# Routing from sums of tokens, scalings gathered in the output's stage, and a reordered first group: a fused audio layer on one core

## Chip, cores, metric

One core of a Trainium2 chip. The metric is the device time of one execution in microseconds (us). All runs quoted for a time were fast, that is, none was over 1.5% above the fastest of its kernel.

## The reference, cut

Sixty-four recordings of 80,000 samples are cut into 157 frames of 512, turned by a cosine transform, and pass one layer: an attention-like mixing with a gate, then a mixture of 16 experts, where each recording takes one expert, chosen from the mean of its tokens. All is fp32.

```python
h = einsum('bfh,kh->bfk', frames, dct)                      # 64 x 157 x 512
x = layernorm(h)
#   phases from tanh(x @ Wk), tanh(x @ Wq); V = x @ Wv; causal sums; gate = sigmoid(x @ Wg)
h = h + x + (gate * total + (1 - gate) * pos) / norm @ Wo + bo
x = layernorm(h)
scores = softmax(mean(x, axis=1) @ Wg + bg)                 # over tokens, then route
idx = argmax(scores); gate = scores[idx]
h = h + gate * (x @ We[idx] + be[idx])
```

## The kernel before

The kernel works through 16 groups of four recordings. A group's tokens are five tiles of 128 (the last is called TAIL); the frames lie turned in `xT` (feature by token). A stage of one group runs beside stages of its neighbours: the value stage of group g holds the routing of g-1, the expert stage of g-1 holds the embedding of g+1.

The frames are turned into values without layernorm's division by the deviation. So each token's column of `xT` must be multiplied by its 1/deviation (`rstd`) before the projections. `rstd` has one value per partition (token); a transpose of it, repeated 128 times, puts it along the free dimension of all partitions ("spread"), and VectorE multiplies ("scale"):

```python
# cut below: s = S[g] (the tiles of group g) and blank lines
def spread(g, n, room=None):
    s["by", n] = tr = bank()[:, :P] if room is None else room
    nc.tensor.transpose(tr, s["rstd", n].to_broadcast([P, P]), ident)

def scale(g, n):
    x, tr = tile_of(s["xT"], n), s.pop(("by", n))
    nc.vector.tensor_tensor(x, x, tr.unsqueeze(1).to_broadcast([P, C, P]), ALU.mult)

def expert(g, n, between=lambda c: None, spreads=()):       # 4 chunks of 4 recordings
    ps = psum()
    for c in range(C):
        between(c); expert_chunk(g, n, c, ps[:, 0, :])
    between(C)
    for k, m in enumerate(spreads):
        spread(g + 2, m, ps[:, 1, P * k : P * (k + 1)])
    expert_out(g, n, ps[:, 0, :])
    for m in spreads:
        scale(g + 2, m)
```

The routing multiplies every token by the routing weights and sums afterwards:

```python
def route(g):
    s["each"] = ps = bank()
    for c in range(C):
        for b in range(GB):                                  # four recordings, four column groups
            nc.tensor.matmul(ps[Q*b : Q*(b+1), :L], rwg[:, c, :], s["x2T"][:, c, b, :L],
                             start=(c == 0), stop=(c == C - 1))
def route_sum(g):
    nc.vector.tensor_reduce(tot, s.pop("each")[:, :L], AX.X, ALU.add)
```

PSUM, into which TensorE writes its products, is used as a ring of four buffers of two banks. Line numbers in the profile lines are those of each kernel's own text; below, the transposes of `rstd` are L290 before and L296 after, their scalings on VectorE L296 and L835 before and L302 after, experts L785 and L814, routing L691 and L706, attention's read L605 and L611. In a line of TensorE, `128*32` is rows and columns of the weights, `128x512` the data that stream past them, `x32` how many instructions are merged; what stands in brackets is the idle time before it and who ended it.

## Time and profile before

| | before |
|---|---|
| time, median | 1418.8 us |
| TensorE busy | 99% |
| VectorE, GpSimd, ScalarE busy | 71%, 42%, 28% |
| one group's period | 85.84 us |
| of it value, gate, expert, read and output stage | 21.79, 16.38, 24.02, 23.65 us |

TensorE is never free in the steady groups; the last two rows are distances between first instructions of stages on TensorE. The lines themselves are in the prediction.

### The profile page before, as it was taken

To read this page: it belongs to the slowest core of one execution; us is meant where nothing else is said; L and a number is where in the kernel's file an instruction comes from. 1 tells how busy PE (TensorE), PEld (TensorE's weight loads), DVE (VectorE), ACT (ScalarE), POOL (GpSimd) and SP (SyncE) were. 2 spreads that over 40 slices of the span, in tenths; PEclk is the share of its full clock that TensorE was granted. 3 is DMA by queue.
4 is the path that set the end of the run, shared out by engine and by line. 5 is a ranking of instruction groups with operands and counts; after the bars stand their busy time and mean duration, and the time that the engine had idled before them with its cause. 6 is when DMAs were issued, how large, how long until landed. Compare 5 with 4: busy or idle time off the path is not lost.

```text
span 1419.2 us, 26967 instructions
## 1 busy us (share of the span) xinstructions
PE 1404.2 (99%) x10647; PEld 929.9 (66%) x10647; DVE 1002.4 (71%) x2091; ACT 401.5 (28%) x690; POOL 602.9 (42%) x846
## 2 busy tenths in 40 slices
PE   9999999999999999999999999999999999999998
PEld 5577575675757667575675757657586675766762
DVE  5777776767767676777777767677676777767574
ACT  2414242141422314232142422314223142421410
POOL 2354534535544255533535445255442545335312
PEclk9999999999999999999999999999999999999999
DMA  6013205032140323204132040322303232030305
GB/s 219 1 38 126 75 1 182 20 127 75 51 139 12 132 69 118 84 1 173 29 127 75 13 173 16 127 75 77 117 8 137 64 126 75 1 141 24 127 8 192
DMA packets 47486, 119.74 MB, mean 84 GB/s; under 512 B 9265, under 2 KB 26177, under 8 KB 39425
## 3 DMA queue, kind: packets, MB, share of 16 engines
q0 software_dynamic: 11072, 71.31, 13.0%
q1 hardware_dynamic: 35788, 46.06, 11.0%
q8 instruction: 85, 1.39, 0.4%
q10 hardware_dynamic: 500, 0.64, 0.2%
q14 instruction: 41, 0.33, 0.1%
HBM read 97.41 MB, written 20.58 MB: 83 GB/s over the span
## 4 chain that ended last, share of the span: by engine, by line
PE 90%; DVE 3%; POOL 3%; issue 1%; DMA 1%; ACT 1%; SPq 0%; DVEq 0%; POOLq 0%
PE mm L364 27%; PE mm L571 16%; PE mm L785 16%; PE mm L605 9%; PE mm L235 8%; PE mm L681 3%; PE mm L516 3%; PE mm L250 2%; PE mm L252 2%; POOL rstd L227 1%; PE mm L691 1%; PE mm L590 1%; DVE st L222 1%; PE mm L290 1%; POOL rstd L226 1%
## 5 line engine op out<-in xcount | busy, mean ns | idle before, releaser
L226 POOL TENSOR_SCALAR rstd<-mv 128x1 f32<-128x1 f32 x160 | 53.1, 332 | 545.9 <-DVE mv L224 539.6
L785 PE MATMUL mm<-we,x2T 128*32 128x512 f32 x2400 | 273.2, 595 | 0.0
L785 PEld LDWEIGHTS mm<-we,x2T 128*32 128x32 f32 x2400 | 70.3, 109 | 148.6 <-issue 141.3
L97 DVE TENSOR_TENSOR gT<-mm,gT 128x128 f32<-128x128 f32 (+1 forms) x135 | 87.0, 672 | 88.5 <-PE mm L571 87.0
L613 DVE TENSOR_TENSOR gT<-mm,gT 128x320 f32<-128x320 f32 x256 | 116.8, 487 | 20.7 <-PE mm L605 16.2
L605 PE MATMUL mm<-att,v 32*128 32x192 f32 (+2 forms) x2048 | 129.1, 374 | 1.1 <-ACT res_t L279 1.1
L605 PEld LDWEIGHTS mm<-att,v 32*128 32x128 f32 x2048 | 107.1, 187 | 11.7 <-PE mm L605 3.0
L739 POOL DMA_INDIRECT we<-in_we,rows x60 | 64.3, 1072 | 105.1 <-issue 98.0
L97 DVE TENSOR_TENSOR v<-mm,v 128x512 f32<-128x512 f32 x105 | 70.9, 688 | 52.9 <-PE mm L364 52.9
L581 ACT ACTIVATE gT<-gT,hbg 128x320 f32<-128x320 f32 x120 | 59.6, 554 | 169.0 <-DVE gT L97 169.0
L227 POOL TENSOR_TENSOR rstd<-rstd,power 128x1 f32<-128x1 f32 x160 | 98.2, 614 | 13.3
L97 DVE TENSOR_TENSOR res<-mm,res 128x512 f32<-128x512 f32 x96 | 64.4, 684 | 54.1 <-POOL res L621 39.2
L279 ACT ACTIVATE res<-mm,shift,rstd 128x512 f32<-128x512 f32 x64 | 49.8, 778 | 161.9 <-POOL rstd L265 126.3
L668 ACT ACTIVATE x<-res,shift,rstd 128x512 f32<-128x512 f32 x64 | 52.0, 814 | 137.8 <-DVE res L97 121.4
L364 PE MATMUL mm<-t_o,sum 128*128 128x256 f32 x384 | 88.3, 379 | 0.4 <-DVE sum L96 0.4
L364 PE MATMUL mm<-t_v,sum 128*128 128x256 f32 x360 | 86.7, 384 | 0.0
L284 POOL TENSOR_TENSOR res<-res,bo 128x512 f32<-128x512 f32 x64 | 86.3, 1379 | 0.2 <-issue 0.2
L796 DVE SCALAR_TENSOR_TENSOR res<-mm,gate,res 128x512 f32<-128x512 f32 x64 | 48.0, 750 | 49.3 <-PE mm L290 36.3
L364 PEld LDWEIGHTS mm<-t_o,sum 128*128 128x128 f32 x384 | 71.9, 190 | 11.6 <-PE mm L364 0.8
L621 POOL TENSOR_TENSOR res<-res,u 128x512 f32<-128x512 f32 x45 | 55.9, 1269 | 42.1 <-DVE u L97 42.1
L235 PE MATMUL mm<-wv,xT 128*128 128x512 f32 x160 | 72.0, 594 | 0.0
L364 PEld LDWEIGHTS mm<-t_v,sum 128*128 128x128 f32 x360 | 64.8, 190 | 10.7 <-issue 3.5
(200 smaller groups left out, 2770.5 us busy)
## 6 DMA issues: line engine op xcount, KB each, us to landing
xT<-in_frames SPq DMA_DIRECT2D x32, 640.0 KB, 4.6
out<-res SPq DMA_DIRECT2D x248, 64.0 KB, 1.7
out<-res_t SPq DMA_DIRECT2D x62, 32.0 KB, 1.6
out<-res_t SPq DMA_DIRECT2D x62, 26.0 KB
wv<-in_wv SPq DMA_DIRECT2D x2, 512.0 KB, 5.8
wg<-in_wg SPq DMA_DIRECT2D x1, 1024.0 KB
wo<-in_wo SPq DMA_DIRECT2D x1, 1024.0 KB
we<-in_we,rows POOLq DMA_INDIRECT x60, 8.5
```

Source lines behind the costliest of these rows:

```text
L97: add = lambda *x: nc.vector.tensor_tensor(*x, ALU.add)
L226: nc.gpsimd.tensor_scalar(rstd, mv[:, 1:2], EPS, None, ALU.add)
L227: nc.gpsimd.tensor_tensor(rstd, rstd, power, ALU.pow)
L235: nc.tensor.matmul(ps, tile_of(x[:, c], n), w[:, c, :], start=(c == 0), stop=(c == C - 1))
L284: nc.gpsimd.tensor_tensor(r, r, bo, ALU.add)
L364: nc.tensor.matmul(ps[:, b, :], lhs[:, c, P * b : P * (b + 1)], w[:, c, :], start=(c == 0), stop=(c == 1))
L571: nc.tensor.matmul(ps[:, o, :HN], w[:, c, o * P : (o + 1) * P], rhs[:, c], start=(c == 0), stop=(c == 1))
L581: nc.scalar.activation(to, to, AF.Tanh, bias=hbg[:, c : c + 1], scale=0.5)
L605: nc.tensor.matmul(to, s["v", n][q, c * P : (c + 1) * P], by, start=(n == 0), stop=(n == TAIL))
L613: nc.vector.tensor_tensor(th, r[:, :, n], th, op)
L739: nc.gpsimd.indirect_dma_start(out=ws[b][:, n * k : n * (k + 1)], out_offset=None, in_=of, in_offset=bass.IndirectOffsetOnAxis(ap=rows[:, ...
L785: nc.tensor.matmul(ps[Q * i : Q * (i + 1), :], s["x2T"][:, c, i, Q * n : Q * (n + 1)], s["ws"][i][:, c, :], start=(c == 0), stop=(c == C - 1),
```

## The change

Its intent: take small work off TensorE. (1) VectorE sums each recording's turned tokens, and the routing multiplies two partial sums in place of 157 tokens. (2) The spreads, five a group and lone between expert products, become six transposes in a row in the output stage, with two large scalings. (3) In the first group, gate parts follow each other without spreads between, statistics come ahead of the phasors, and GpSimd's sum of the gate's weights moves back. The last group keeps the token-wise routing (`route_tokens`).

```diff
+    def scale_all(g):
+        ps = psum()
+        lo = 0
+        for n in (0, 1, TAIL, TAIL, 2, 3):
+            rows = slice(0, P) if n != TAIL else slice(0, HT) if lo < HN - 1 else slice(HT, P)
+            ...
+            nc.tensor.transpose(ps[:, m, at : at + w], s["rstd", n][rows].to_broadcast([w, P]), ident[rows, rows])
+            lo += w
+        for m in range(2):
+            x = half(s["xT"], m)
+            nc.vector.tensor_tensor(x, x, ps[:, m, :HN].unsqueeze(1).to_broadcast([P, C, HN]), ALU.mult)
...
+    def token_sum(g, k):
+        lo, hi = ((2 * Q, L), (0, 2 * Q))[k]
+        nc.vector.tensor_reduce(s["xsum"][:, :, k], x[:, :, lo:hi], AX.X, ALU.add)
...
-                    ps[Q * b : Q * (b + 1), :L], rwg[:, c, :], s["x2T"][:, c, b, :L], ...
+                    ps[Q * b : Q * (b + 1), :], rwg[:, c, :], s["xsum"][:, GB * c + b, :], ...
... first_values
-        total = add_up(raw_g, D, "x2T", nc.gpsimd)       # before value(0, 1)
         value(0, 1)
...
+        total = add_up(raw_g, D, "x2T", nc.gpsimd)       # after embed_res(0, 3)
... first_gate: four calls of spread and scale, and the TAIL's, taken out
... project_and_values
         keep_product(g)
+        token_sum(g - 1, 0)
         value_product(g, 6)
         turn_x2(g - 1, 1)
         phasors(g)
         keep_product(g)
-        fold_once(g + 1, 0)      # moves down, to just before value_product(g, 5)
+        token_sum(g - 1, 1)
         value_product(g, 7)
...          # route(g - 1) from before to after value_product(g, 5); value_product(g, 3) ahead of route_spread
... experts_and_embedding
-        expert(g - 1, 0, spreads=(0, 1))
+        expert(g - 1, 0)
-        expert(g - 1, 2, spreads=(2, 3))
+        expert(g - 1, 2)
-        expert(g - 1, 3, spreads=(TAIL,))
+        expert(g - 1, 3)
... attention, after output product 7
+            elif i == 7 and ahead:
+                scale_all(g + 1)
```

More of the change, by code (lines that the diff above doesn't have):

```diff
@@ L284, in add_bo @@
         nc.gpsimd.tensor_tensor(r, r, bo, ALU.add)
-    def spread(g, n, room=None):
+    def scale_all(g):
         s = S[g]
-        s["by", n] = tr = bank()[:, :P] if room is None else room
-        nc.tensor.transpose(tr, s["rstd", n].to_broadcast([P, P]), ident)
-    def scale(g, n):
-        s = S[g]
-        x, tr = tile_of(s["xT"], n), s.pop(("by", n))
-        nc.vector.tensor_tensor(x, x, tr.unsqueeze(1).to_broadcast([P, C, P]), ALU.mult)
+        ps = psum()
+        lo = 0
+        for n in (0, 1, TAIL, TAIL, 2, 3):
+            rows = slice(0, P) if n != TAIL else slice(0, HT) if lo < HN - 1 else slice(HT, P)
+            m, at = divmod(lo, HN)
+            w = rows.stop - rows.start
+            nc.tensor.transpose(
+                ps[:, m, at : at + w], s["rstd", n][rows].to_broadcast([w, P]), ident[rows, rows]
+            )
+            lo += w
+        for m in range(2):
+            x = half(s["xT"], m)
+            nc.vector.tensor_tensor(x, x, ps[:, m, :HN].unsqueeze(1).to_broadcast([P, C, HN]), ALU.mult)
     def quarters(w):
@@ L682, in turn_x2 @@
         copy(s["x2T"][:, :, :, Q * n : Q * (n + 1)], tr.rearrange("p (c b t) -> p c b t", c=C, b=GB))
+    def token_sum(g, k):
+        s = S[g]
+        if k == 0:
+            s["xsum"] = p2.tile([P, C * GB, 2], F32, tag="xsum", name="xsum")
+        x = s["x2T"].rearrange("p c b t -> p (c b) t")
+        lo, hi = ((2 * Q, L), (0, 2 * Q))[k]
+        nc.vector.tensor_reduce(s["xsum"][:, :, k], x[:, :, lo:hi], AX.X, ALU.add)
     def route(g):
         s = S[g]
-        s["each"] = ps = bank()
+        s["each"] = ps = bank()[:, :2]
         for c in range(C):
@@ L691, in route, with route_tokens @@
                 nc.tensor.matmul(
-                    ps[Q * b : Q * (b + 1), :L], rwg[:, c, :], s["x2T"][:, c, b, :L], start=(c == 0), stop=(c == C - 1)
+                    ps[Q * b : Q * (b + 1), :],
+                    rwg[:, c, :],
+                    s["xsum"][:, GB * c + b, :],
+                    start=(c == 0),
+                    stop=(c == C - 1),
+                )
+    def route_tokens(g):
+        s = S[g]
+        s["each"] = ps = bank()[:, :L]
+        for c in range(C):
+            for b in range(GB):
+                nc.tensor.matmul(
+                    ps[Q * b : Q * (b + 1), :], rwg[:, c, :], s["x2T"][:, c, b, :L], start=(c == 0), stop=(c == C - 1)
                 )
@@ L697, in route_sum @@
         s["tot"] = tot = p2.tile([P, 1], F32, tag="tot", name="tot")
-        nc.vector.tensor_reduce(tot, s.pop("each")[:, :L], AX.X, ALU.add)
+        nc.vector.tensor_reduce(tot, s.pop("each"), AX.X, ALU.add)
     def route_spread(g):
@@ L801, in expert_out, with expert @@
                 queue.dma_start(out=out[GB * g + i, Q * n + lo : Q * n + hi, :], in_=o[Q * i + lo : Q * i + hi, :])
-    def expert(g, n, between=lambda c: None, spreads=()):
+    def expert(g, n, between=lambda c: None):
         ps = psum()
@@ L809, in expert @@
         between(C)
-        for k, m in enumerate(spreads):
-            spread(g + 2, m, ps[:, 1, P * k : P * (k + 1)])
         expert_out(g, n, ps[:, 0, :])
-        for m in spreads:
-            scale(g + 2, m)
-    def scale_all(g):
-        s = S[g]
-        ps = psum()
-        for m in range(2):
-            lo = 0
-            for n, w, at in ((0, P, 0), (1, P, 0), (TAIL, HT, 0)) if m == 0 else ((TAIL, HT, HT), (2, P, 0), (3, P, 0)):
-                nc.tensor.matmul(
-                    ps[:, m, lo : lo + w],
-                    s["rstd", n].to_broadcast([P, P]),
-                    ident[:, at : at + w],
-                    start=True,
-                    stop=True,
-                )
-                lo += w
-        for m in range(2):
-            x = half(s["xT"], m)
-            nc.vector.tensor_tensor(x, x, ps[:, m, :HN].unsqueeze(1).to_broadcast([P, C, HN]), ALU.mult)
     def first_values():
@@ L884, in first_values @@
         keep_value(0, 2)
+        next(consts)
+        value(0, 3)
         mean_g = bank()
@@ L887, in first_values @@
         centre(raw_g, mean_g, D)
-        value(0, 3)
         value(0, TAIL)
         keep_value(0, 3)
-        next(consts)
         keep_value(0, TAIL)
@@ L903, in first_values @@
         fold_phases(0)
-        phasors(0, (0,))
-        next(consts)
-        next(consts)
         embed(1, 0)
         embed_statistics(1, 0)
+        next(consts)
+        phasors(0, (0,))
+        embed_res(1, 0)
         phasors(0, (1,))
-        embed_res(1, 0)
+        next(consts)
         next(consts)
@@ L919, in weights @@
             next(made)
-        def deviations(n):
-            spread(1, n)
-            scale(1, n)
         gate_part(0, 0)
@@ L927, in first_gate @@
         embed_statistics(1, 1)
+        weigh()
         embed_res(1, 1)
-        weigh()
         fold_twice(1, 1)
-        deviations(0)
         add_bo(0, 0)
@@ L937, in first_gate @@
         embed_statistics(1, 2)
-        deviations(1)
         embed_res(1, 2)
@@ L947, in first_gate @@
             embed_res(1, n)
-        deviations(2)
         add_bo(0, 2)
@@ L951, in first_gate @@
         gate_part(0, 3)
-        add_bo(0, 3)
-        deviations(3)
-        deviations(TAIL)
-        add_bo(0, TAIL)
+        for n in (3, TAIL):
+            add_bo(0, n)
         weights()
@@ L989, in project_and_values @@
         next(weights, None)
+        fold_once(g + 1, 0)
+        value_product(g, 5)
         route(g - 1)
+        keep_product(g)
         route_sum(g - 1)
-        value_product(g, 5)
-        keep_product(g)
         next(weights, None)
         next(weights, None)
+        value_product(g, 3)
         route_spread(g - 1)
+        keep_product(g)
         pick(g - 1)
@@ L1002, in project_and_values @@
         keep_value(g, TAIL)
-        value_product(g, 3)
-        keep_product(g)
         value_product(g, 4)
@@ L1121, in routes @@
         elif c == 3:
-            route(g)
+            route_tokens(g)
             route_sum(g)
```

## The prediction

> **What bounds the kernel now.** I read the page first: the busy line, then the shares of the chain that ended last.
>
> ```profile
> span 1419.2 us, 26967 instructions
> PE 1404.2 (99%) x10647; PEld 929.9 (66%) x10647; DVE 1002.4 (71%) x2091; ACT 401.5 (28%) x690; POOL 602.9 (42%) x846
> ...
> PE 90%; DVE 3%; POOL 3%; issue 1%; DMA 1%; ACT 1%; SPq 0%; DVEq 0%; POOLq 0%
> ```
>
> TensorE has 15 us without work in the whole span, and the chain runs on it for 90%. So a change pays by the TensorE time that it takes out; what it does to VectorE counts only where VectorE would come late. Busy time of pipelined matmuls overlaps, so I cost a piece of TensorE work as the distance from its start to the start of what follows. The timeline of TensorE, for one group of four samples in the middle (starts in us, durations in us):
>
> ```profile
> 574.76 3.64 PE L785 MATMUL mm<-we,x2T 128*32 128x512 f32 x32
> 578.34 0.71 PE L250 MATMUL mm<-dct_e,xT 128*128 128x128 f32 x4
> ...
> 583.89 0.74 PE L290 MATMUL mm<-ident,rstd 128*128 128x128 f32 x2
> 584.47 0.62 PE L250 MATMUL mm<-dct_e,xT 128*128 128x128 f32 x4
> ...
> 594.60 0.43 PE L290 MATMUL mm<-ident,rstd 128*128 128x128 f32 x2
> 594.96 3.64 PE L785 MATMUL mm<-we,x2T 128*32 128x512 f32 x32
> 598.53 0.32 PE L290 MATMUL mm<-ident,rstd 128*128 128x128 f32 x1
> 598.78 1.90 PE L605 MATMUL mm<-att,v 32*128 32x320 f32 x32
> ...
> 627.49 0.60 PE L681 MATMUL mm<-ident,x 128*128 128x128 f32 x4
> 627.92 1.89 PE L364 MATMUL mm<-wv,xT 128*128 128x256 f32 x8
> ...
> 634.08 1.27 PE L691 MATMUL mm<-x2T,rwg 128*32 128x157 f32 x32
> 635.28 1.99 PE L364 MATMUL mm<-t_v,sum 128*128 128x256 f32 x8
> ...
> 660.60 3.64 PE L785 MATMUL mm<-we,x2T 128*32 128x512 f32 x32
> ```
>
> The first and last of these lines are the same work one group apart: a group takes 660.60 - 574.76 = 85.84 us. L290 are the spreads (transposes of rstd) that the change gathers in one place, L691 the routing that it shrinks, L681 ordinary transposes, four in a row.
>
> The second place is the first group's gate stage, by the table of stretches (length, then busy time by engine; the column after POOL is the granted clock):
>
> ```profile
> 57.38:81.49 24.11, 19.63 (x127) 14.18 (x125) 18.22 (x41) 9.04 (x16) 12.47 (x27) 1.00 0.02 2
> 81.49:107.36 25.87, 25.87 (x224) 21.51 (x225) 18.44 (x33) 2.03 (x3) 14.67 (x14) 0.93 0.15 51
> 107.36:193.20 85.84, 85.74 (x660) 57.18 (x659) 63.92 (x134) 24.79 (x43) 37.54 (x52) 1.00 0.24 83
> ```
>
> In 57.38 to 81.49 TensorE stands still for 24.11 - 19.63 = 4.5 us, against 0.1 us in a whole later group, and in the next stretch its clock is cut (0.93).
>
> **What the Trainium skill says.** "TensorE: Matmul & The Clock Gate", "Wait — 56ns, not 53.3ns?": two matmuls never start closer than about 25 ns, however few columns. This trace does not agree for products on four column groups: the last eight of a score product (L590, 32 columns each) start 7 ns apart in fours, and the second four 28 ns after the first (563.627 and 563.655 us). The same page, Part 4, gives about 275 to 390 ns for one transpose in another data type. A lone L290 here costs 0.25 us, but four L681 in a row cost 627.92 - 627.49 = 0.43 us, so 0.11 us each: a run of transposes is cheaper than lone ones. Part 1 says that an idle window of some 3.4 us halves the clock; the 0.93 after the stalled stage agrees in kind. "VectorE: DVE Perf Modes", the perf-mode tier table, gives tensor_reduce no faster mode than one element a cycle; the trace has 220 ns for 64 elements (L717) and 321 ns for 157 (L698), a slope of 1.09 ns and about 150 ns fixed, which agrees.
>
> **The change part by part.**
>
> 1. Spreads out of the expert stage, in each of 14 groups. Removed: 583.89 to 584.47 is 0.58, less 0.08 because L250 directly after L785 takes 0.54 to its successor and here 0.46, so 0.50; 594.60 to 594.96 is 0.36; 598.53 to 598.78 is 0.25, of which I keep 0.05 for a dearer changeover. Sum 1.06 us, times 14 = **-14.8 us**.
>
> 2. Six transposes in a row in the output stage, for 15 groups (two of them of 64 columns, which I count full, as the weights loaded are as wide): 6 x 0.11 = 0.66, with a trifle for changeover 0.68 us, times 15 = **+10.2 us**. For the first group, twelve passes of an ordinary product (L825, 1.34 us on the chain) become six transposes: **-0.65 us**.
>
> 3. Routing from sums. Now 32 matmul instructions (each fp32 product shows as two) take 635.28 - 634.08 = 1.20 us, and the products on either side lose 0.1 each at the changeover from 128 to 32 columns. After it the count is the same with 2 columns in place of 157. These are eight rounds of four; a round takes 133 ns now, and 28 ns for 32 columns. I take 30 to 40 ns a round for 2 columns, 0.3 us, and keep the changeovers. Saved 0.8 us, a little under the 0.9 that this gives, times 15 = **-12.0 us**. The last group keeps the token-wise routing.
>
> 4. VectorE pays for it with two reductions, of 16 x 93 = 1488 and 16 x 64 = 1024 elements: by the slope 1.7 and 1.2 us, less 0.17 for the shorter final reduction, +2.75 us a group, 41 us in the run. Five scalings of 0.68 (L296, 3.2 us with their drains overlapped) become two of 1.48 (L835): no gain to speak of in work, but they move. All this lies beside TensorE if it arrives in time. In the value stage (622.4 to 644.2) VectorE is busy 17.3 of 21.8 us and waits 1.07, 1.15 and 1.57 us for products of TensorE (L364), 3.8 us to fill with 2.75. Following the new order by hand, the sums end near 12.4 us after the stage's start and route comes at 13.3, as route now stands behind one more product. In the output stage:
>
> ```profile
> 617.45 0.69 DVE L97 TENSOR_TENSOR u<-mm,u 128x512 f32<-128x512 f32 x1 [0.44 <-PE mm L364]
> 620.76 1.29 DVE L97 TENSOR_TENSOR res<-mm,res 128x512 f32<-128x512 f32 x2 [2.62 <-POOL res L621]
> ```
>
> VectorE waits 2.62 us for GpSimd exactly where the change sets 2 x 1.48 = 2.96 us. It comes 0.34 us later, TensorE 0.66 us later: nothing is lost. **0 us.**
>
> 5. The first gate stage. The four lone spreads and their waits between gate parts go, each frees a buffer of four in PSUM, and the first embedding's statistics move ahead of the phasors. At most 4.5 us idle and 1.0 us of spreads can go, and if the clock is no longer cut, 2.3 us more (the first read of attention, L605, takes 10.32 us on the chain against 8.02 in later groups). The chain there goes through ScalarE, VectorE and GpSimd, so not all is freed; I take **-5.2 us**.
>
> Sum: -14.8 + 10.2 - 0.65 - 12.0 - 5.2 = -22.4; 1418.7 - 22.4 = 1396 us.
>
> **The rivals.** (a) Routing of 2 columns costs nearly what it did, because issue or weight loads set its pace (25 ns for each of 32 is 0.8 us, the skill's floor): then part 3 gives 0.4 x 15 = 6 us, and the time is 1402. For it: nothing in this kernel has so few columns. Against it: the 28 ns rounds. (b) VectorE comes late in the value stage: the sums are in front of evictions that free PSUM buffers, and of the pick that starts the fetch of expert weights, about 1 us later. Transfers of the fetch end near 655 us and their use starts at 660.6, so 5 us are in hand; against it too are VectorE's waits counted above. If it fails, 0.5 to 1 us a group come back: 1404 to 1411. (c) The two long scalings hold up the evictions of the output stage and then the statistics, of whose last links (normal2, turn) TensorE waits already on the edge (a transpose at 625.26 starts just after its input's end at 625.17): 0.3 us a group, 1401. (d) Everything fits and the first stage loses all its idle time: 1391.
>
> **Range and chances.** The saving per group is 1.18 us by the sum, with 0.3 either way for routing and 0.3 downward for VectorE; over 15 groups 4 to 9 us. The first stage adds 3 either way. So 1388 to 1406. The line of 2% is 1390.3: to be beyond it routing must be nearly free and the first stage give all. Faster 0.12, same 0.86, slower 0.02.
>
> **What would show it.** Right: a group's period near 84.7 us, TensorE still 99% busy; no spreads between expert products; L290 six times in a row over about 0.66 us in the output stage; routing 0.3 to 0.5 us from its start to the next product; VectorE some 40 us busier; the first gate stage short by 4 to 6 us and the clock after it whole. Wrong: routing still near 1 us (rival a), new idle time of TensorE on VectorE in the value stage (b) or in the output stage (c), or a period that does not fall by the removed work, which would mean that a lone spread between expert products had cost less than its distance shows.

## The result and the profile after

The changed kernel takes 1396.8 us (median of 4, 1396.3 to 1397.5) against 1418.8. The ratio is 0.9844 (95% interval 0.9827 to 0.9861); here and below a ratio is the mean time of one kernel's fast runs over that of the other's of the same rounds, so not quite the ratio of the medians. The gain is 22.0 us, 1.6%: by the line of 2% that the prediction draws, the same, to which it had given 0.86.

From the page of the changed kernel, the busy line and the chain:

```profile
span 1395.0 us, 26923 instructions
PE 1383.8 (99%) x10656; PEld 919.3 (66%) x10656; DVE 1033.5 (74%) x2076; ACT 399.7 (29%) x690; POOL 598.8 (43%) x846
...
PE 96%; DMA 1%; ACT 1%; DVE 1%; POOL 1%; issue 0%; SPq 0%; POOLq 0%; DVEq 0%; ACTq 0%
```

TensorE is still the bound; it has 20.4 us less to do. VectorE has 31 us more, and that cost nothing visible. The timeline of TensorE for one group (start, duration, engine, line, operation):

```profile
561.80 3.64 PE L814 MATMUL mm<-we,x2T 128*32 128x512 f32 x32
565.37 0.71 PE L250 MATMUL mm<-dct_e,xT 128*128 128x128 f32 x4
...
577.57 7.07 PE L814 MATMUL mm<-we,x2T 128*32 128x512 f32 x64
584.57 1.90 PE L611 MATMUL mm<-att,v 32*128 32x320 f32 x32
...
603.04 0.94 PE L296 MATMUL mm<-ident,rstd 128*128 128x128 f32 x6
603.82 1.89 PE L370 MATMUL mm<-t_o,gT 128*128 128x256 f32 x8
...
622.38 0.43 PE L706 MATMUL mm<-xsum,rwg 128*32 128x2 f32 x32
622.74 1.99 PE L370 MATMUL mm<-wv,sum 128*128 128x256 f32 x8
...
646.34 3.64 PE L814 MATMUL mm<-we,x2T 128*32 128x512 f32 x32
```

The period is 646.34 - 561.80 = 84.54 us, 1.30 less. The routing takes 0.36 us to the next product (1.20 before); the six transposes 0.78 us. By stages, from first instruction to first instruction (means over the groups, rounded):

| stage of a steady group | before | after | difference |
|---|---|---|---|
| value (with the routing) | 21.79 | 20.95 | -0.84 |
| gate | 16.38 | 16.38 | 0 |
| expert (spreads gone) | 24.02 | 22.77 | -1.25 |
| read and output (six transposes) | 23.65 | 24.43 | +0.78 |

Where VectorE was to fit in, it does. Its timeline, at the two places that the prediction named:

```profile
604.02 2.88 DVE L302 TENSOR_TENSOR xT<-xT,mm 128x1280 f32<-128x1280 f32 x2
606.83 1.35 DVE L97 TENSOR_TENSOR res<-mm,res 128x512 f32<-128x512 f32 x2
...
617.11 1.69 DVE L698 TENSOR_REDUCE xsum<-x2T 128x16 f32<-128x1488 f32 x1
...
619.65 1.22 DVE L698 TENSOR_REDUCE xsum<-x2T 128x16 f32<-128x1024 f32 x1 [0.24 <-ACT x2T L688]
```

The two scalings stand exactly where VectorE had waited 2.62 us for GpSimd, and the line after them has no wait left. The second sum ends at 620.87, and the routing starts on TensorE at 622.38.

In the first groups the second group's value stage starts at 101.4 us after the span's start, against 107.4. That profiled run of before was 2.3 us above its median, so this difference is not yet the gain; the experiments settle it.

### The profile page after: what moved, and what is told of

Read it like the earlier page. It is cut to its first block, busy times and chain, and to the rows that moved or that the text cites. A ratio compares the mean times of both kernels' runs of the same rounds, so it can differ in the third digit from the quotient of the medians.

```text
span 1395.0 us, 26923 instructions
## 1 busy us (share of the span) xinstructions
PE 1383.8 (99%) x10656; PEld 919.3 (66%) x10656; DVE 1033.5 (74%) x2076; ACT 399.7 (29%) x690; POOL 598.8 (43%) x846
## 4 chain that ended last, share of the span: by engine, by line
PE 96%; DMA 1%; ACT 1%; DVE 1%; POOL 1%; issue 0%; SPq 0%; POOLq 0%; DVEq 0%; ACTq 0%
PE mm L370 27%; PE mm L814 20%; PE mm L577 16%; PE mm L611 9%; PE mm L235 9%; PE mm L250 3%; PE mm L687 3%; PE mm L522 3%; PE mm L252 2%; PE mm L596 1%; PE mm L296 1%; PE mm L196 1%; DMA t_v<-in_we,rows 1%; DMA wv<-in_wv 0%; PE mm L706 0%
## 5 line engine op out<-in xcount | busy, mean ns | idle before, releaser
L814 PE MATMUL mm<-we,x2T 128*32 128x512 f32 x2400 | 270.3, 595 | 0.0
L619 DVE TENSOR_TENSOR gT<-mm,gT 128x320 f32<-128x320 f32 x256 | 116.8, 487 | 28.7 <-PE mm L611 24.3
L119 POOL TENSOR_TENSOR xT<-xT 128x640 f32<-128x640 f32 x30 | 46.8, 1559 | 91.6 <-DVE even L97 84.7
L97 DVE TENSOR_TENSOR v<-mm,v 128x512 f32<-128x512 f32 x105 | 70.7, 686 | 18.8 <-PE mm L370 18.4
L370 PE MATMUL mm<-t_v,sum 128*128 128x256 f32 x360 | 82.7, 379 | 0.0
L284 POOL TENSOR_TENSOR res<-res,bo 128x512 f32<-128x512 f32 x64 | 79.8, 1275 | 0.0
L370 PEld LDWEIGHTS mm<-t_o,sum 128*128 128x128 f32 x384 | 71.9, 190 | 11.7 <-PE mm L370 0.8
L97 DVE TENSOR_TENSOR res<-mm,res 128x512 f32<-128x512 f32 x96 | 65.2, 685 | 15.0 <-ACT u L630 11.8
```

What stands on the lines that cost most here:

```text
L97: add = lambda *x: nc.vector.tensor_tensor(*x, ALU.add)
L284: nc.gpsimd.tensor_tensor(r, r, bo, ALU.add)
L370: nc.tensor.matmul(ps[:, b, :], lhs[:, c, P * b : P * (b + 1)], w[:, c, :], start=(c == 0), stop=(c == 1))
L619: nc.vector.tensor_tensor(th, r[:, :, n], th, op)
L814: nc.tensor.matmul(ps[Q * i : Q * (i + 1), :], s["x2T"][:, c, i, Q * n : Q * (n + 1)], s["ws"][i][:, c, :], start=(c == 0), stop=(c == C - 1),
```

## The experiments

The first four take the change apart. They ran on one chip in the same rounds; times are medians of four runs, three of them in rounds with the kernel before (1418.9). The later ones are from other rounds, in which the kernel before took 1418.8 to 1418.9, and the last two from another chip; they are set beside the 1396.8 of the changed kernel all the same.

### Routing from sums alone

```diff
 # the kernel before, with the changed kernel's token_sum, route and order of the value stage
-    ps[Q*b : Q*(b+1), :L], rwg[:, c, :], s["x2T"][:, c, b, :L]
+    ps[Q*b : Q*(b+1), :],  rwg[:, c, :], s["xsum"][:, GB*c + b, :]
```

> The kernel before with the routing from sums alone, and the new order of the value stage that goes with it. Theory (TensorE is the bound and VectorE arrives in time, so the terms add up): the value stage is shorter by 0.83 us in each of 15 groups, as the profile of the changed kernel shows (21.79 to 20.96 us), 12.5 us in all: about 1406. Rival (the sums make VectorE late and other parts of the change pay for it): less than 8 us, 1411 or more, with new idle time of TensorE in the value stage.

Measured: 1406.5 us, ratio 0.9909 (0.9893 to 0.9926), 12.4 us less. The value stage takes 20.95 us and the other three are as before. The theory's number holds, and the rival falls. The new order of the stage is in this run too, but gains nothing by itself: with it and the routing by tokens ("Sums made, but not used" below) the stage takes 21.79 us as before.

### Scalings at one place alone

```diff
 # the kernel before; groups 2 to 15
-        expert(g - 1, 0, spreads=(0, 1))        # and (2, 3), (TAIL,)
+        expert(g - 1, 0)
+            elif i == 7 and ahead and g > 0:
+                scale_turned(g + 1)             # six transposes, two scalings
```

> The kernel before with the scalings of groups 2 to 15 at one place in the output stage; routing and first group as before. Theory: 1.25 us less in the expert stage and 0.78 us more in the output stage, 0.47 us in each of 14 groups, 6.6 us in all: about 1412. My prediction had 1.06 less and 0.68 more, 0.38 a group, 5.3 us. Rival (the two long scalings keep VectorE from the evictions, hidden in the full change by the routing): 0 to 3 us, 1416 to 1419.

Measured: 1412.6 us, ratio 0.9951 (0.9935 to 0.9968), 6.3 us less. Expert stage 22.77, read and output 24.43, the others as before: a period of 85.38 us. Nothing was hidden by the routing.

### The first group alone

```diff
 # the kernel before, with the changed kernel's first_values, first_gate and scale_all for groups 0 and 1
+            elif i == 7 and g == 0:
+                scale_all(g + 1)
```

> The kernel before with the first group's part alone: new order of the first values and the first gate, and the scalings of the first two groups by six transposes. Theory: all of the first 6 us up to the second group, less some 2 us by which the profiled run of before was slower than its median: 1413 to 1415. With e1 and e2 it should add up to the 22 us of the whole change within 1.5 us; if the sum is clearly more or less, the parts help or hinder one another.

Measured: 1415.1 us, ratio 0.9973 (0.9957 to 0.999), 3.8 us less. The three parts sum to 12.4 + 6.3 + 3.8 = 22.5 us, the whole change gives 22.0: they add up to within 0.5 us, as expected (within 1.5).

The first group's own account can be read between this run and the routing run, whose first group is that of before. To the first transposes of rstd 39.93 against 41.85 us; from there to attention's read 35.15 against 39.10; the read and output stage of the first group 26.25 against 24.20. So 1.9 and 4.0 us are gained, and 2.05 given back, of which 0.78 are the new transposes of the second group. The rest, 1.26 us, is a longer read (9.84 us in place of 8.58), with a new wait inside. The timeline of TensorE, first of the routing run and then of this run:

```profile
80.95 2.09 PE L605 MATMUL mm<-att,v 32*128 32x320 f32 x26 [1.28 <-ACT res_t L279]
```

```profile
75.08 2.05 PE L605 MATMUL mm<-att,v 32*128 32x320 f32 x29
...
78.19 2.09 PE L605 MATMUL mm<-att,v 32*128 32x320 f32 x26 [0.73 <-ACT res_t L279]
```

The read now starts earlier than the last tile's statistics are through ScalarE, so part of the wait that stood before the read moved into it.

### Sums made, but not used

```diff
 # the changed kernel
-        route(g - 1)
+        route_tokens(g - 1)      # token_sum stays
```

> The changed kernel with the sums still made on VectorE, but routing by all 157 tokens, so that the sums are work without use (the result stays right). Theory: VectorE's 2.9 us a group are free, so only TensorE's 0.83 us a group come back: 1396.8 + 12.5 = 1409.3. Rival (the sums delay TensorE somewhere): more than 12.5 us come back, 1412 or above, as the longer route then also waits.

Measured: 1408.6 us, ratio 0.9925 (0.9909 to 0.9942), 11.8 us more than the changed kernel. With VectorE's sums made for nothing, no more comes back than TensorE's work for 157 tokens. VectorE's 2.9 us a group are free here. Of the 0.7 us under the expected number 0.4 are in the second group: there VectorE also makes the gate's weight sums in the value stage, and with routing from sums the routing's result waits behind them (first period 84.92 in place of 84.54 us in the changed kernel, here 85.38 as in all later groups). The routing run has this loss too. The rest is within what two profiled runs differ by at their ends (0.5 us between these two).

### Five transposes in place of six

```diff
-        for n in (0, 1, TAIL, TAIL, 2, 3):       # TAIL as two pieces of 64 rows
-            nc.tensor.transpose(ps[:, m, at : at + w], s["rstd", n][rows]..., ident[rows, rows])
+        ps = psum().rearrange("p m n -> p (m n)")
+        for k, n in enumerate((0, 1, TAIL, 2, 3)):
+            nc.tensor.transpose(ps[:, P * (k + 1) : P * (k + 2)], s["rstd", n].to_broadcast([P, P]), ident)
         for m in range(2):
+            lo = P + HN * m
-            ... ps[:, m, :HN] ...
+            ... ps[:, lo : lo + HN] ...
```

> The changed kernel with five full transposes in a row in place of six of which two are of 64 rows; they lie end to end over two banks of PSUM, and the second scaling reads across the border. Theory (a change between 128 and 64 rows makes TensorE drain: the two 64-row transposes start 203 ns after the one before, and the next 200 ns after them, against 107 ns between full ones): the run takes 0.54 us in place of 0.78, 0.24 us in each of 16 places, 3.8 us: 1393.0. Rival (each transpose costs the same 0.11 to 0.13 us): 0.13 us each, 2 us: 1394.8.

Measured: 1392.6 us, ratio to before 0.9811 (0.9798 to 0.9824), 4.2 us below the changed kernel's median; against before, the interval holds the line of 2%, so whether this is beyond it stays unclear. The timeline of TensorE:

```profile
601.17 0.71 PE L291 MATMUL mm<-ident,rstd 128*128 128x128 f32 x5
601.71 1.89 PE L362 MATMUL mm<-t_o,gT 128*128 128x256 f32 x8
```

Five take 601.71 - 601.17 = 0.54 us, 0.11 each; six had taken 0.78. The period falls by 0.24 to 84.30. So the two short transposes were dear, not because there was one more of them (in the changed kernel's trace the two start 0.004 us apart) but because going to 64 rows and back each costs about 0.1 us. This is what I had counted as "full". The Trainium skill, "TensorEngine Tiling (Array Packing)", Key Properties, says that a change of tiling mode drains TensorE; the changed kernel's trace agrees in that 0.20 us pass from the start of a full transpose to that of a half one, against 0.11 between full ones. I had not looked the page up for the prediction.

### The same scalings at the end of the expert stage

```diff
-            elif i == 7 and ahead:
+            elif i == 7 and g == 0:
                 scale_all(g + 1)
 # experts_and_embedding
         expert(g - 1, 3)
+        scale_all(new)
```

> The changed kernel with the six transposes and two scalings moved from the output stage to the end of the expert stage, just ahead of attention's read; same instructions, another place. Theory (the place matters because VectorE waits 2.62 us for GpSimd in the output stage, while in the read stage it is nearly full): VectorE comes about 1 us late to the read, the four PSUM buffers run out and TensorE waits, 0.5 to 1.5 us in each of 14 groups: 1404 to 1418. Rival (only the count of TensorE's work matters): 1397, as the changed kernel.

Measured: 1415.6 us, ratio to before 0.9976 (0.9959 to 0.9992), 18.8 us above the changed kernel: nearly the whole gain is lost by a place. The period is 85.83 us. Timeline of TensorE in the read stage:

```profile
594.08 0.76 PE L611 MATMUL mm<-att,v 32*128 32x320 f32 x4
595.33 1.40 PE L611 MATMUL mm<-att,v 32*128 32x320 f32 x22 [0.49 <-DVE xT L302]
```

and of VectorE at the same place:

```profile
592.30 2.88 DVE L302 TENSOR_TENSOR xT<-xT,mm 128x1280 f32<-128x1280 f32 x2
595.10 1.93 DVE L619 TENSOR_TENSOR gT<-mm,gT 128x320 f32<-128x320 f32 x4
```

TensorE has filled the PSUM buffers and waits for VectorE, which is at the scalings (L302) until 595.18 and begins to take the read's products out of PSUM (L619) only at 595.10. The read and output stage takes 24.80 us although its six transposes are gone, against 24.43 with them; 24.43 - 0.78 would be 23.65, so 1.15 us a group are stall. Besides, the transposes are dearer here: the expert stage grows by 0.93 us with them (22.77 to 23.70), not by 0.78. Together 1.15 + 0.93 - 0.78 = 1.30 us a group. The "0 us" of the prediction's fourth step thus held because of the place, not because two scalings are little.

### GpSimd's sum of the gate's weights put back

```diff
 # first_values of the changed kernel
         fold_once(0, 1, nc.vector)
         fold_twice(0, 1)
+        total = add_up(raw_g, D, "x2T", nc.gpsimd)
         value(0, 1)
 ...
-        total = add_up(raw_g, D, "x2T", nc.gpsimd)      # after embed_res(0, 3)
```

> The changed kernel with GpSimd's sum of the gate's weights put back where the kernel before had it, beside VectorE's subtraction of the second half of the first group. Theory (the two slow each other down: the subtraction took 2.85 us beside that sum and 0.82 without it): the subtraction goes back to about 2.8 us, TensorE waits for it about 1 us before the third embedding, and 1 to 2 us come back: 1398 to 1399. Rival (the 2.85 us had another cause, such as the loads in flight): 1396.8 and the subtraction stays at 0.82 us.

Measured: 1398.2 us, ratio to before 0.9852 (0.9836 to 0.9869), 1.4 us above the changed kernel. Timelines of all engines at this place, first this run and then the changed kernel:

```profile
21.77 0.82 DVE L97 TENSOR_TENSOR even<-xT 128x640 f32<-128x640 f32 x1
21.82 2.98 POOL L203 TENSOR_TENSOR total<-wg 128x1024 f32<-128x1024 f32 x1
...
22.62 2.86 DVE L119 TENSOR_TENSOR xT<-xT 128x640 f32<-128x640 f32 x1
```

```profile
22.41 0.82 DVE L119 TENSOR_TENSOR xT<-xT 128x640 f32<-128x640 f32 x1
```

Beside GpSimd's sum (21.82 to 24.80) VectorE's subtraction of two SBUF operands ends at 25.48, which is 24.80 plus little less than its own 0.82; and GpSimd's sum takes 2.98 in place of 2.35 us, which fits its having first stood behind VectorE's addition (to 22.59). TensorE then waits 1.02 us for the folded frames. The Trainium skill says this in "SBUF — State Buffer", "SBUF: two separate sides": an instruction of VectorE with two SBUF inputs and one of GpSimd that reads SBUF exclude each other for their whole length. The trace agrees, with the 25.48 us above. In the prediction I had given this move nothing.

### Two experts end to end

```diff
 # on top of the five transposes
         add_bias(g - 1, TAIL)
-        expert(g - 1, TAIL)
         embed(new, 0)
         embed(new, 1)
         embed_statistics(new, 0)
         embed_statistics(new, 1)
+        expert(g - 1, TAIL)
         add_bias(g - 1, 0)
```

> The kernel with five transposes, and besides the first two embeddings of the next group ahead of the first expert product in place of between the first and the second, so that the two expert products stand end to end. Theory (the spreads between expert products cost more than I counted because each change between 32 and 128 columns makes TensorE drain: two expert products end to end take 7.00 us, 0.15 less than two with other work between): from the gate's last product to the third embedding 0.23 to 0.33 us less in each of 14 groups, 3 to 5 us: 1388 to 1389.5. Rival (the 0.15 us is only how the trace splits neighbouring products): within 1 us of the 1392.6 of the five transposes.

Measured: 1387.9 us (1387.6 to 1388.3), ratio to before 0.9781 (0.9768 to 0.9795): the fastest of all, and clearly over 2% faster than the kernel before. The period falls by 0.34 us from that of the five transposes to 83.96, a little more than the 0.23 to 0.33 expected. Timeline of TensorE:

```profile
559.49 0.61 PE L252 MATMUL mm<-trig_o,xT 128*128 128x129 f32 x4
560.03 7.07 PE L806 MATMUL mm<-we,x2T 128*32 128x512 f32 x64
```

The same products, in another order, with one pair of changeovers less: 0.34 us a group. It is not an artefact of how the trace splits neighbours, as the time falls by it.

### Routing on 32 columns

```diff
-                    s["xsum"][:, GB * c + b, :],
+                    s["x2T"][:, c, b, :Q],       # 32 tokens; wrong routing on purpose
```

> The changed kernel with routing from 32 token columns in place of 2 columns of sums; the routing is wrong on purpose, only the pace matters. Theory (loading 32 columns of weights for each of the four column groups sets the pace of a round at 27 to 32 ns, not the columns of data): routing takes 0.32 to 0.40 us to the next product as with 2 columns (0.36), and the period stays at 84.5 us. Rival (columns of data still count): 32 columns of 0.85 ns add 27 ns a round, 0.2 us a group, 84.75 us.

The result is wrong, as meant. One look (1397.1 us, state unknown), in the timeline of TensorE:

```profile
622.95 0.46 PE L706 MATMUL mm<-x2T,rwg 128*32 128x32 f32 x32
623.34 1.99 PE L370 MATMUL mm<-wv,sum 128*128 128x256 f32 x8
```

0.39 us with 32 columns, 0.36 with 2, and a period of 84.56: the data hardly count any more. That is what is left of the routing when its data are next to nothing; that the load of 32 columns of weights sets this pace fits, but is not separated here from a limit on issue.

## Why the prediction was right, point by point

The time (1396.8 for 1396) and the mechanism hold: TensorE is the bound, what is taken from it comes off the time, and VectorE's new work fits in. But the sum is better than its terms: their errors cancel, and that the total came so close is in part luck.

- **Spreads out, -14.8 predicted.** Measured 1.245 us a group, 14 x 1.245 = -17.4. Two terms were mis-sized. I counted only the 0.36 us of the two spreads that stood between two experts, but with them gone the experts themselves became shorter: two end to end take 584.57 - 577.57 = 7.00 us, against 3.58 + 3.57 = 7.15 before, so 0.15 us of the changeover had been counted as time of the experts. And the 0.05 that I kept for the last spread was not needed. The order experiment shows that this changeover is real.
- **Transposes in, +10.2 predicted.** Measured 0.78 us, 15 x 0.78 = +11.7. I took six of 0.11, two of them "of 64 columns"; in the trace these have 64 rows, and cost about 0.2 us more together, for changeovers, as the five-transpose run shows. For the first group -0.56 (predicted -0.65).
- **Routing, -12.0 predicted.** Measured -12.4 alone; 0.84 a group. The rounds of four took 32 ns, inside the 30 to 40 that I took after the 28 of the score products. Rival (a), a floor of 25 ns a matmul, falls: 32 matmuls in 0.36 us are 11 ns each.
- **VectorE, 0 predicted.** Right: the unused sums bring back only TensorE's own work, and the scalings sit in its 2.62 us of waiting. Rivals (b) and (c) fall here, except for 0.4 us once, in the second group. The move to the expert stage's end shows that the danger of (c) is real at another place: it takes 18.8 us. VectorE became 31 us busier, not some 40: the sums cost what was forecast (1.69 + 1.22 us a group), but two large scalings take 2.88 us where five small ones took 3.2, and in the first group VectorE is rid of 2 us of waiting inside its subtraction.
- **First group, -5.2 predicted, beside the -0.65.** Too much. The experiment with this part alone gains 3.8 us with the second group's transposes in it, so 3.8 + 0.78 - 0.56 = 4.0 without the two. And only half of it comes from where it was sought: 1.9 us were gained before the first transposes, 1.4 of them by a move that I gave nothing, GpSimd's sum away from VectorE's subtraction. From there to the read 3.95 - 0.56 = 3.4 were gained, of which 1.3 came back inside the read, as the same tile was waited for there. (The gate stage had five lone spreads, not four.) Rival (d), no idle time left there, falls: 2.5 us of waits remain (1.2, 0.7 and 0.6). The step that failed is "if the clock is no longer cut, 2.3 us more": the cut was of that one profiled run. There the clock stood at half from 82.66 to 86.07 us, and the first read and output stage took 25.88 us in place of 24.20, so the cut cost 1.7 of the 2.3 us by which that run was above the median. The runs with routing alone and scaling alone have the same first group, the same 4.5 us of standing still, and a clock of 1.00 in the stretch after; here that of routing alone:

```profile
81.00:105.00 24.00, 24.00 (x224) 19.80 (x225) 18.22 (x33) 1.99 (x3) 14.61 (x14) 1.00 0.17 55
```

What cut the clock stays open: before the cut TensorE never stood still for longer than 1.47 us at a time in that stage, which is not the idle window of some 3.4 us that the prediction quotes.

Together: -17.4 + 11.7 - 0.56 - 12.4 - 4.0 = -22.7, measured -22.0; the 0.4 us of the second group are inside the -12.4. The 0.7 us left over are no more than profiled runs with the same work at their ends differ by (39.6 to 40.3 us up to the first transposes of `rstd` in seven runs, 71.9 to 72.4 us from the last read on in all but one). Measured less predicted, term by term: -2.6 (spreads), +1.5 (transposes), +0.1 and +1.2 (first group), -0.4 (routing).

## What to carry to other kernels

Where TensorE is full, cost a piece of its work by the distance between starts and count the changeovers with it: here a lone transpose cost 0.25 us where in a run of its like it costs 0.11, and putting like next to like gained 0.34 us a group without removing anything. Moved work on another engine was free at a place where that engine waited for something else, and took nearly the whole gain at one where it did not; look for that wait first, and give the work to it. Take a clock cut or a stall from one profile as the run's own until a second run shows it.

## What the Trainium skill lacked or had wrong

- "TensorE: Matmul & The Clock Gate", "Wait — 56ns, not 53.3ns?": a floor of about 25 ns between starts of matmuls, without an exception. On four column groups 32 matmuls of 2 columns took 0.36 us, 11 ns each, and 32 of 32 columns 0.39 us. Part 3 of the same page does have starts of some 4 ns apart for products on different tiles of the array; here they are 7 ns apart within a round of four, while the rounds, so the starts on one and the same column group, stay 28 to 32 ns apart. So the floor is to be read for one tile.
- The same page, Part 4: about 275 to 390 ns for a transpose, measured in another data type. The time of one agrees (fp32, 128 x 128: 276 ns in a row on L681, 312 ns for the lone ones on L290, means of the kernel before). What it lacks is the distance in a row: 0.11 us from start to start (five in 0.54 us).
- "TensorEngine Tiling (Array Packing)", Key Properties: names the drain at a change of tiling mode, but gives no size. Here 0.24 us for going to 64 rows and back amid full transposes (0.78 against 0.54 us, with one transpose more), and 0.34 us for one pair of changes between 32 and 128 columns.
- "SBUF — State Buffer": agrees; a size: 0.82 to 2.86 us for VectorE's fp32 subtraction of 640 columns beside GpSimd's sum.
